# Moving small DMAs between queues and slots: where the B/C matrix is stored, and when its rows and the convolution strips are fetched

## The chip, the cores and the metric

The kernel runs on one core of a Trainium2 chip. A core has five engines, each with its own instruction stream: TensorE (PE in the profile; PEld is its weight load), VectorE (DVE), ScalarE (ACT), GpSimd (POOL) and SyncE (SP), which here only issues DMAs. Every stream runs in order and waits on semaphores that other streams or landed DMAs raise. The metric is the device time of one execution in microseconds; the kernel before takes 27,648.13 us (median of three runs, 27,644.12 to 27,659.78).

## The reference

The input is 8 images of 64 channels and 128x128 pixels, float32. Layer 0 runs a bidirectional selective scan (Mamba) over every row and over every column, averages the four results, normalises by groups of channels and adds the input. Layer 1 is a residual block of two 3x3 convolutions with batch normalisation. The scan of one sequence, cut to what matters:

```
x, z  = split(in_w @ seq);  x = silu(causal_conv(x))
dt, B, C = split(xp_w @ x)            # B and C: 16 states each
delta = softplus(dt_w @ dt + dt_b)
for t:                                # per channel d (128) and state n (16)
    h[d,n] = exp(delta[t,d] * A[d,n]) * h[d,n] + delta[t,d] * x[t,d] * B[t,n]
    y[t,d] = sum_n h[d,n] * C[t,n]
y = (y + x * D) * silu(z);  out = out_w @ y
```

Forward and reversed sequences give `f` and `r`, and the layer takes 0.5 * (f + r).

## The kernel before, in words

**Units and slots.** The work of layer 0 is cut into 512 units: 8 images, for each 32 units of four rows (`o == 0`, units 0 to 31 of an image) and 32 units of four columns (`o == 1`, units 32 to 63). A unit has 512 time steps times 128 channels times 16 states times 2 directions. It is cut into 16 slots `r`; a slot treats 64 channels (`half`), 4 states (`ng`) and one direction (`d`), so that 128 partitions hold 32 channels times 4 states and two channel quarters lie side by side: tiles of 128x1024. `where(r)` gives half, state group and direction.

**What a slot does.** `decay` (ScalarE, L350): a copy of zeros at the sequence edges and two Exp of 128x508 give `dA` in PSUM; there are two such tiles, so a slot's decay waits for the scan two slots back. `drive` (L362): `s = du * B`, on VectorE with B in PSUM (`pb`, made by TensorE in `b_rows`), or, in slots 2, 5, 9, 12 and 15 (`GPS`), on GpSimd with B in an SBUF tile `bt` that a DMA fetched (`b_tile`). `scan` (VectorE, L370): the recurrence as one instruction. `weigh` (GpSimd, L379): `s = s * C`, with C in an SBUF tile `c`. `add_up` (TensorE) folds the states, four slots later.

**What feeds a unit.** `prepare(g, before)` is a generator that makes the next unit's inputs in pieces, one piece in each of slots 0 to 6 and 8 to 13 of the current unit. Piece 9 (slot 9) makes `du = delta * x` on VectorE (L287) and `dl = delta` on ScalarE and stores both to DRAM with eight DMAs of 128 KB (`keep`, L282). Pieces 10 to 13 read them back, replicated over the four states: `replicate(g, half, d)` (L314) issues two loads of 512 KB, one `dl` and one `du`, into a pool of five tiles each. The order is (0,0), (1,0), (0,1), (1,1), in slots 10 to 13. In slot 11 ScalarE copies B and C out of PSUM (`bc`, L299) and SyncE stores that tile of 128 KB to DRAM (`bd`, L301), ahead of the second pair. From `bd` come the `bt` tiles (256 KB, a row broadcast to 32 partitions) and the `c` tiles. `c_rows` (L329) loads both directions of a state group at once: four loads of 512 KB per unit into two tiles.

**Order.** The main loop (L538 on) is written out by hand; nothing reorders it. A wait that heads SyncE's queue holds everything behind it. In the kernel before, `fetch(s + 7)` issues a `bt` load seven slots ahead and `fetch_c(s + 3)` a `c` load three slots ahead of its first use. In slot order SyncE's queue is thus: slot 9, the eight stores and a `c`; 10, first pair; 11, `bd`, second pair, `bt` of slot 2; 12, third pair; 13, fourth pair and a `c`; 14, `bt` of slot 5; then 1, `c`; 2, `bt`; 5, `bt` and `c`; 8, `bt`. The `bt` of slot 2 is the first load that reads the new `bd`.

**Normalisation and first convolution.** They run inside the row units of the next image. `normalize` (units 1 to 16) takes 512 columns per unit: slot 5 loads `xr`, slot 7 adds on GpSimd (L443) and SyncE stores `x1_d` (L444). `conv1` makes one output tile per unit from unit 5 on, in slots 14, 15, 0, 1 and 2: three groups of matmuls, the copy and store of the result (`cs`, L488 and L489), statistics. Its input strips (two SBUF tiles, two or more loads of x1_d rows each, `strip_of`) are loaded one tile ahead, at the start of the tile before, in slot 14. After the last image both run outside the loop (L590 to L597), then come the second convolution and the output.

Of the kernel before, what the change touches and what calls it, by code (L numbers as in the profile page):

```python
# [9 lines left out]
F32 = mybir.dt.float32  # L10
# [5 lines left out]
P = 128  # L16
# [3 lines left out]
N = 512  # L20
# [12 lines left out]
def tile_mamba2d_then_resblock(ctx: ExitStack, tc: tile.TileContext, x, par, gn, p_w, o_w, new_p, bn, cst, out):  # L33
# [169 lines left out]
    with ExitStack() as st:  # L203
# [42 lines left out]
        def prepare(g, before):  # L246


            w = wt[g["o"]]
            if g["o"] == 1:  # L250
                g["xc"] = work.tile([P, SEQ, HH], F32, name="xc", bufs=1)
                i = SEQ * g["i"]
                nc.scalar.copy(g["xc"], xt.rearrange("p h w -> p w h")[:, i : i + SEQ, :])
            yield
            cp = psm.tile([P, 2, N], F32, name="cp", tag="pt")
            for d in range(2):
                for s in range(NTAP):
                    j = NTAP - 1 - s
                    project(
                        cp[:, d, :], [w["wc"][:, 0, j, :], w["wc"][:, 1, j, :]], g,  # L260
                        s if d == 0 else -s, s == 0, s == NTAP - 1,
                    )
                    if s % 2:
                        yield
            u = work.tile([P, 2, N], F32, name="u")
            nc.scalar.activation(u, cp, AF.Silu, bias=w["conv_b"])  # L266
            if before is not None:
                nc.scalar.activation(before["sz"], before["sz"], AF.Silu)
            g["u"] = u
            yield  # L270
            dp = psm.tile([P, 2, N], F32, name="dp", tag="pt")
            for d in range(2):
                nc.tensor.matmul(dp[:, d, :], w["wd"], u[:, d, :], start=True, stop=True)  # L273
            yield
            nc.scalar.activation(dp, dp, AF.Softplus, bias=w["dt_b"])
            yield
            dd = g["dd"] = scratch.tile([2, 2, 32, NQ, N], F32, name="dd")

            def keep(k, v):

                for q in range(NQ):
                    nc.sync.dma_start(  # L282
                        out=dd[k, :, :, q, :].rearrange("d c t -> c d t"), in_=v[32 * q : 32 * (q + 1)]
                    )

            du = work.tile([P, 2, N], F32, name="du", tag="nat")
            nc.vector.tensor_mul(du, dp, u)  # L287
            dl = work.tile([P, 2, N], F32, name="dl", tag="nat")
            nc.scalar.copy(dl, dp)  # L289
            keep(1, du)  # L290
            keep(0, dl)
            yield
            bp = psm.tile([P, 2, N], F32, name="bp", tag="pt")
            for d in range(2):
                nc.tensor.matmul(bp[0 : 2 * NS, d, :], w["wbc"], u[:, d, :], start=True, stop=True)  # L295
            replicate(g, 0, 0)
            yield
            bc = work.tile([2 * NS, 2, N], F32, name="bc", tag="nat")
            nc.scalar.copy(bc, bp[0 : 2 * NS])  # L299
            bd = scratch.tile([2 * NS, 2, N], F32, name="bd")  # L300
            nc.sync.dma_start(out=bd, in_=bc)  # L301
            g["bd"] = bd
            replicate(g, 1, 0)
            yield
            replicate(g, 0, 1)
            yield
            zp = psa.tile([P, N], F32, name="zp", tag="b")
            project(zp, [w["wz"][:, 0, :], w["wz"][:, 1, :]], g, 0, True, True)
            g["sz"] = work.tile([P, N], F32, name="sz")
            nc.scalar.copy(g["sz"], zp)  # L310
            replicate(g, 1, 1)
            yield
# [13 lines left out]
            ng, k = divmod(r, 4)  # L326
            return k % 2, ng, k // 2

        def c_rows(g, ng):  # L329

            t = rep.tile([P, 2, N], F32, name="c", bufs=2)
            src = g["bd"][NS + 4 * ng : NS + 4 * ng + 4].rearrange("n d t -> n (d t)")
            nc.sync.dma_start(out=t.rearrange("p d t -> p (d t)"), in_=src.partition_broadcast(32))
            g["c", ng] = t

        def b_tile(g, r):

            half, ng, d = where(r)
            t = rep.tile([P, N], F32, name="bt", bufs=3)
            nc.sync.dma_start(out=t, in_=g["bd"][4 * ng : 4 * ng + 4, d, :].partition_broadcast(32))  # L340
            g["bt", r] = t
# [36 lines left out]

        def weigh(g, r):  # L379
            half, ng, d = where(r)  # L380
            s, c = g["s", r], g["c", ng][:, d, :]
            nc.gpsimd.tensor_mul(s, s, c.unsqueeze(1).to_broadcast([P, 2, N]))  # L382

        def skip(g):
# [62 lines left out]
        def strip_of(b, t, k):  # L447

            x1 = x1_d[b].rearrange("p (h w) -> p h w", w=W)
            strip = strips[k % 2]  # L450
            for e in range(2):
                es = slice(e * C, (e + 1) * C)
                rows = [2 * SEQ * t + 2 * j - e for j in range(SEQ + 1)]
                for hf in range(2):
                    js = [j for j, r in enumerate(rows) if hf * HH <= r < (hf + 1) * HH]
                    if js:
                        r = rows[js[0]] - hf * HH
                        nc.sync.dma_start(
                            out=strip[es, js[0] : js[-1] + 1, 1 : W + 1],
                            in_=x1[hf * C : (hf + 1) * C, r : r + 2 * len(js) - 1 : 2, :],  # L460
                        )

                if rows[0] < 0:
                    nc.vector.memset(strip[es, 0, :], 0.0)
                if rows[-1] >= W:
                    nc.vector.memset(strip[es, SEQ, :], 0.0)

        def conv1(b):


            order = [0, 1, 9, 2, 10, 3, 11, 4, 12, 5, 13, 6, 14, 7, 15, 8]
            strip_of(b, order[0], 0)
            st1 = small.tile([P, NT, 6], F32, name="st1", bufs=1)
            yield
            for k, t in enumerate(order):
                if k + 1 < NT:
                    strip_of(b, order[k + 1], k + 1)
                ps = psm.tile([P, 2, N], F32, name="cps", tag="pt")[:, 0, :]
                for kw in range(3):
                    for blk in range(2):  # L480
                        nc.tensor.matmul(  # L481
                            ps.rearrange("p (r w) -> p r w", w=W), w1[:, blk, kw, :],
                            strips[k % 2][:, blk : blk + SEQ, kw : kw + W],
                            start=(kw == 0 and blk == 0), stop=(kw == 2 and blk == 1),
                        )
                    yield
                cs = work.tile([P, N], F32, name="cs", tag="tok", bufs=3)
                nc.scalar.copy(cs, ps)  # L488
                nc.sync.dma_start(out=c1_d[b][:, t * N : (t + 1) * N], in_=cs)  # L489
                yield  # L490
                nc.vector.bn_stats(st1[:, t, :], cs)
                if k == NT - 1:
                    nc.sync.dma_start(out=st1_d[:, b], in_=st1)
                yield
# [16 lines left out]
        def at(s):  # L511
            return gs[s // UN], s % UN

        def fetch(s):
            if s < total and s % UN in GPS:
                b_tile(*at(s))

        def fetch_c(s):
            if s < total and s % 4 == 0:
                g, r = at(s)  # L520
                c_rows(g, where(r)[1])

        def ahead(r):

# [2 lines left out]
        with tc.manual_schedule():  # L527
            load_image(0)
            for _ in prepare(gs[0], None):
                pass  # L530
            fetch_c(0)
            fetch_c(4)
            for s in range(7):
                fetch(s)
            decay(*at(0))
            b_rows(*at(0))
# [1 line left out]
            for s in range(total + UN):  # L538
# [20 lines left out]
                    nc.scalar.activation(gs[n]["sz"], gs[n]["sz"], AF.Silu)  # L559
                if s % 2 == 0 and s + 2 < total:  # L560
                    b_rows(*at(s + 2))
                if r in CONV and n % PER > 5 or r >= CONV[0] and n % PER == 5:
                    next(conv3, None)
                if r in PREP:
                    next(pieces, None)
# [3 lines left out]
                    add_up(*at(s - LAG))  # L569
                if r in NORM and n % PER:  # L570
                    next(norm, None)
                fetch(s + 7)
                fetch_c(s + 3)
                if r == OUT and prev:
                    if n % PER == 5:
                        next(conv3, None)
                    output = emit(prev)
                    next(output)
                elif r == OUT + 1:
                    next(output, None)  # L580
                    if n % PER == 0 and prev:
                        for _ in conv3:
                            pass
                        norm = normalize(prev["b"], stats.pop(prev["b"]))
                        next(norm)
                        conv3 = conv1(prev["b"])
                elif r == 8 and live and n % PER == PER - 2 and gs[n]["b"] + 1 < B:
                    load_image(gs[n]["b"] + 1)
# [152 lines left out]
```

## Time and profile before

One profiled execution took 27,638.15 us, of which the span from the first to the last instruction is 27,636.0 us.

| what | value |
|---|---|
| median of three runs | 27,648.13 us |
| profiled execution, its span | 27,638.15 us, 27,636.0 us |
| VectorE busy | 26,018.6 us (94%) |
| GpSimd busy | 25,128.0 us (91%) |
| PE matmul busy | 19,347.3 us (70%) |
| ScalarE busy | 18,349.8 us (66%) |
| DMA | 4871.45 MB, mean 176 GB/s; SyncE's queue 52.8% of the 16 DMA engines' time |
| scan, each (L375, L377) | 2278 and 2280 ns, 8192 in all |
| drive on VectorE (L367) | 1200 ns, 5632 in all |
| drive on GpSimd (L367) | 2365 ns, 2560 in all |
| weigh on GpSimd (L382) | 2364 ns, 8192 in all |

Busy time is a union, so overlapping ends of neighbours count once. The idle time in a group's row is what its engine waited just before those instructions, with what ended most of it. A row "X <- DMA a<-b" means that the last thing to arrive was that load. SyncE (SPq) has no busy time; its waits are told by a view of their own.

### The profile page before, as it was taken

What the parts mean: (1) busy time and instruction counts of PE and PEld (TensorE: products, weight loads), DVE (VectorE), ACT (ScalarE), POOL (GpSimd) and SP (SyncE); (2) the same over time, 40 slices, a digit from 0 to 9 for tenths busy, and PEclk for the clock granted to TensorE, in tenths of its full rate; (3) what the DMA queues carried; (4) which work ended last, traced back from release to release, by engine and by line L of the source; (5) the groups of instructions that cost most, each with busy time, mean ns of one, the idle gap of its engine ahead of it and who ended that gap; (6) DMA issues with size and microseconds to landing.
All of it is one profiled execution on the core that took longest, in us unless ns stands there. A gap on an engine that the chain in (4) does not pass through costs nothing.

```text
span 27636.0 us, 232983 instructions
## 1 busy us (share of the span) xinstructions
PE 19347.3 (70%) x65068; PEld 6675.0 (24%) x65068; DVE 26018.6 (94%) x16145; ACT 18349.8 (66%) x30638; POOL 25128.0 (91%) x10916
## 2 busy tenths in 40 slices
PE   6766677666776667766676667766677666776676
PEld 1222222222222222222222222222222222222222
DVE  8999999999999999999999999999999999999942
ACT  5766666666676666766667666666667666666632
POOL 7999999999999999999999999999999999999930
PEclk8888888888888888888888888888888888888888
DMA  5555555555555555555555555555555555555545
GB/s 177 173 173 173 177 183 180 173 174 178 185 175 173 172 182 185 175 173 170 183 185 173 174 176 178 184 171 176 175 185 182 170 176 176 186 176 171 172 141 188
DMA packets 1861563, 4871.45 MB, mean 176 GB/s; under 512 B 240272, under 2 KB 387872, under 8 KB 1844384
## 3 DMA queue, kind: packets, MB, share of 16 engines
q1 hardware_dynamic: 1839664, 4754.93, 52.8%
q10 hardware_dynamic: 15984, 68.06, 0.9%
q0 software_dynamic: 4608, 33.56, 0.3%
q8 instruction: 513, 8.40, 0.1%
q14 instruction: 794, 6.50, 0.1%
HBM read 4116.04 MB, written 738.98 MB: 176 GB/s over the span
## 4 chain that ended last, share of the span: by engine, by line
DVE 40%; issue 21%; PE 17%; DMA 10%; ACT 8%; POOL 2%; SPq 1%; DVEq 0%; POOLq 0%; ACTq 0%
DVE s L367 14%; DVE s L375 12%; DVE s L377 10%; DMA du<-dd 7%; PE pb L347 6%; ACT dA L358 4%; PE yp L398 3%; PE cps L650 2%; PE dp L273 2%; PE bp L295 2%; DVE du L287 2%; POOL s L382 1%; DVE y L405 1%; DMA bt<-bd 1%; PE cp L241 1%
## 5 line engine op out<-in xcount | busy, mean ns | idle before, releaser
L382 POOL TENSOR_TENSOR s<-s,c 128x1024 f32<-128x1024 f32 x8192 | 19121.0, 2364 | 1104.3 <-DMA c<-bd 440.6
L358 ACT ACTIVATE dA<-dl,A 128x508 f32<-128x508 f32 x16384 | 11274.9, 688 | 616.4 <-DMA dl<-dd 101.1
L347 PE MATMUL pb<-u,wb 128*128 128x512 f32 x8192 | 5419.6, 748 | 7657.6 <-DVE s L367 7313.1
L377 DVE TENSOR_TENSOR_SCAN s<-dA,s 128x1024 f32<-128x1024 f32 x4096 | 9296.2, 2280 | 52.3 <-ACT dA L358 40.5
L375 DVE TENSOR_TENSOR_SCAN s<-dA,s 128x1024 f32<-128x1024 f32 x4096 | 9287.2, 2278 | 0.0
L367 DVE TENSOR_TENSOR s<-du,pb 128x1024 f32<-128x1024 f32 x5632 | 6757.8, 1200 | 559.0 <-DMA du<-dd 452.1
L367 POOL TENSOR_TENSOR s<-du,bt 128x1024 f32<-128x1024 f32 x2560 | 6055.3, 2365 | 317.3 <-DMA bt<-bd 140.6
L355 ACT COPY dA<-zeros 128x8 f32<-128x8 f32 x8192 | 1349.0, 165 | 6360.6 <-DVE s L377 4676.1
L398 PE MATMUL yp<-s,fold 128*32 128x512 f32 x32768 | 5386.2, 671 | 5.3 <-POOL s L382 5.3
L347 PEld LDWEIGHTS pb<-u,wb 128*128 128x128 f32 x8192 | 1468.9, 216 | 10579.4 <-DVE s L367 5372.1
L235 PE MATMUL cp<-xt,wc 128*128 128x512 f32 (+3 forms) x4096 | 2063.2, 628 | 132.7 <-DMA xt<-x_h 76.0
L241 PE MATMUL cp<-xc,wc 128*128 128x256 f32 (+3 forms) x8192 | 2095.3, 401 | 0.0
L241 PEld LDWEIGHTS cp<-xc,wc 128*128 128x128 f32 x8192 | 1607.4, 202 | 1038.2 <-issue 459.6
L398 PEld LDWEIGHTS yp<-s,fold 128*32 128x32 f32 x32768 | 821.7, 115 | 3451.8 <-issue 2080.6
L295 PE MATMUL bp<-u,xpT 128*32 128x512 f32 x2048 | 1636.7, 948 | 4.8 <-ACT dl L289 4.8
L358 ACT ACT_TABLE_LOAD x1030 | 1321.5, 1283 | 20.3 <-DMA dl<-dd 2.3
L235 PEld LDWEIGHTS cp<-xt,wc 128*128 128x128 f32 x4096 | 782.2, 202 | 1469.4 <-issue 1116.2
L273 PE MATMUL dp<-u,wd 128*128 128x512 f32 x2048 | 1017.3, 621 | 1.2 <-ACT u L266 1.2
L299 ACT COPY bc<-bp 32x1024 f32<-32x1024 f32 x512 | 513.1, 1002 | 744.4 <-PE yp L398 677.0
L388 PE MATMUL yp<-u,dg 128*128 128x512 f32 x2048 | 961.9, 592 | 1.2 <-DVE y L405 1.2
L679 POOL DMA_DIRECT2D out<-cc x32 | 17.2, 537 | 975.6 <-ACT cc L678 975.6
L481 PE MATMUL cps<-strip,w 128*128 128x512 f32 x1536 | 754.4, 618 | 134.3 <-DMA strip<-x_d 128.0
(107 smaller groups left out, 10117.9 us busy)
## 6 DMA issues: line engine op xcount, KB each, us to landing
c<-bd SPq DMA_DIRECT2D x2049, 512.0 KB, 4.8
dl<-dd SPq DMA_DIRECT2D x2048, 512.0 KB, 6.5
du<-dd SPq DMA_DIRECT2D x2048, 512.0 KB, 7.4
bt<-bd SPq DMA_DIRECT2D x2560, 256.0 KB, 4.7
dd<-du SPq DMA_DIRECT2D x2048, 128.0 KB, 2.3
dd<-dl SPq DMA_DIRECT2D x2048, 128.0 KB, 2.4
bd<-bc SPq DMA_DIRECT2D x512, 128.0 KB, 5.4
c_d<-cs SPq DMA_DIRECT2D x256, 256.0 KB, 5.2
```

The lines of the kernel that those rows point to most:

```text
L235: nc.tensor.matmul(ps[:, :, lo:hi], lhsT[hf], xt[:, r : r + SEQ, lo - s : hi - s], start=start, stop=stop)
L241: nc.tensor.matmul(ps[:, :, lo:hi], lhsT[hf], g["xc"][:, :, lo - s - hf * HH : hi - s - hf * HH], start=start and hf == 0, stop=stop and h ...
L273: nc.tensor.matmul(dp[:, d, :], w["wd"], u[:, d, :], start=True, stop=True)
L295: nc.tensor.matmul(bp[0 : 2 * NS, d, :], w["wbc"], u[:, d, :], start=True, stop=True)
L347: nc.tensor.matmul(pb, wt[g["o"]]["wb"][:, P * ng : P * (ng + 1)], g["u"][:, d, :], start=True, stop=True)
L355: nc.scalar.copy(dA[:, :, :, edge], zeros)
L358: nc.scalar.activation(dA[:, j, :, t], dl[:, j, :, t], AF.Exp, scale=wt[g["o"]]["A"][:, 2 * half + j, ng : ng + 1])
L367: engine.tensor_mul(s, g["du", half, d], b.unsqueeze(1).to_broadcast([P, 2, N]))
L375: nc.vector.tensor_tensor_scan(s, a, s, 0.0, ALU.mult, ALU.add)
L377: nc.vector.tensor_tensor_scan(s[:, ::-1], a[:, ::-1], s[:, ::-1], 0.0, ALU.mult, ALU.add)
L382: nc.gpsimd.tensor_mul(s, s, c.unsqueeze(1).to_broadcast([P, 2, N]))
L398: nc.tensor.matmul(g["yp"][32 * q : 32 * (q + 1), :], fold, s[:, j, :], start=False, stop=r == UN - 2, skip_group_check=True,)
```

## The change

Four edits:

- B and C are stored to DRAM by ScalarE's DMA queue, behind the copy that makes them, and no longer by SyncE.
- `c` comes in eight loads of 256 KB per unit, one per state group and direction, into five tiles of half the size (before: four of 512 KB into two).
- `fetch` places all `bt` and `c` loads: `bt` of slot 2 six slots ahead (slot 12, behind the third replica pair; before: slot 11), `bt` of slot 5 four slots ahead (slot 1; before: slot 14), the other three as before. `c` of slots 0 and 2 four slots ahead (slots 12 and 14), the other six five slots ahead (slots 15, 1, 3, 5, 7 and 9).
- The convolution starts one unit later (unit 6, slot 12, where two strips are loaded); from then on a strip is loaded two tiles ahead, with the statistics in slot 2.

The order of instructions on GpSimd is unchanged; on TensorE and VectorE only the convolution moves, by one unit; ScalarE gets 512 DMA issues.

```diff
             bd = scratch.tile([2 * NS, 2, N], F32, name="bd")
-            nc.sync.dma_start(out=bd, in_=bc)
+            nc.scalar.dma_start(out=bd, in_=bc)
...
-        def c_rows(g, ng):
-
-            t = rep.tile([P, 2, N], F32, name="c", bufs=2)
-            src = g["bd"][NS + 4 * ng : NS + 4 * ng + 4].rearrange("n d t -> n (d t)")
-            nc.sync.dma_start(out=t.rearrange("p d t -> p (d t)"), in_=src.partition_broadcast(32))
-            g["c", ng] = t
+        def c_rows(g, r):
+
+            half, ng, d = where(r)
+            t = rep.tile([P, N], F32, name="c", bufs=5)
+            src = g["bd"][NS + 4 * ng : NS + 4 * ng + 4, d, :]
+            nc.sync.dma_start(out=t, in_=src.partition_broadcast(32))
+            g["c", ng, d] = t
...
             strip_of(b, order[0], 0)
+            strip_of(b, order[1], 1)
...
-                if k + 1 < NT:
-                    strip_of(b, order[k + 1], k + 1)
...
                 nc.vector.bn_stats(st1[:, t, :], cs)
+                if k + 2 < NT:
+                    strip_of(b, order[k + 2], k + 2)
...
         def fetch(s):
-            if s < total and s % UN in GPS:
-                b_tile(*at(s))
-
-        def fetch_c(s):
-            if s < total and s % 4 == 0:
-                g, r = at(s)
-                c_rows(g, where(r)[1])
+
+
+            for k in range(8):
+                r = (s + k) % UN
+                if s + k < total and r in GPS and k == (6 if r == GPS[0] else 4 if r == GPS[1] else 7):
+                    b_tile(*at(s + k))
+                if s + k < total and r % 2 == 0 and k == (4 if r < 4 else 5):
+                    c_rows(*at(s + k))
...
-                if r in CONV and n % PER > 5 or r >= CONV[0] and n % PER == 5:
+                if r in CONV and n % PER > 6 or r >= CONV[0] and n % PER == 6:
                     next(conv3, None)
...
-                fetch(s + 7)
-                fetch_c(s + 3)
+                fetch(s)
                 if r == OUT and prev:
-                    if n % PER == 5:
+                    if n % PER == 6:
                         next(conv3, None)
```

## The prediction

> **What bounds the kernel now.** I read the page first, then the waits by engine, the busy time by stretch, SyncE's own waits, and last the timeline of single units.
>
> ```profile
> PE 19347.3 (70%) x65068; PEld 6675.0 (24%) x65068; DVE 26018.6 (94%) x16145; ACT 18349.8 (66%) x30638; POOL 25128.0 (91%) x10916
> ...
> L367 DVE TENSOR_TENSOR s<-du,pb 128x1024 f32<-128x1024 f32 x5632 | 6757.8, 1200 | 559.0 <-DMA du<-dd 452.1 <-PE pb L347 83.9 <-PE cp L235 6.5
> ```
>
> VectorE is the bound. In the unit loop its idle time is almost all in one group, the drive, and most of that waits for a `du` load. The waits give the count, and GpSimd's largest:
>
> ```profile
> DVE s L367 <- DMA du<-dd: 452.1, 253, 11.2
> POOL s L382 <- DMA c<-bd: 440.6, 264, 4.3
> ```
>
> Cut to the third image, busy time per stretch (us, PE, PEld, DVE, ACT, POOL, clock, DMA share, GB/s): units 7 to 16, which carry normalisation and convolution, and column units 32 to 62.
>
> ```profile
> 7052.80:7584.10 531.30, 397.15 (x1240) 122.40 (x1240) 499.09 (x301) 362.03 (x611) 497.37 (x220) 0.90 0.59 186
> ...
> 8346.10:9933.80 1587.70, 1083.24 (x4030) 415.72 (x4030) 1580.63 (x990) 1087.97 (x1831) 1513.35 (x653) 0.84 0.53 175
> ```
>
> The column half is full (1580.63 of 1587.70): nothing can be won there. All gain must come from row units. The same cut of the waits puts VectorE's wait for `du` at 3.2 us in units 1 to 4, 2.3 in 5 and 6 (plus 11.1 for TensorE, which stands behind the first strip), 28.7 in 7 to 16, 9.8 in 17 to 21, 10.8 in 22 to 31 and 2.5 in 32 to 62. The first image, without normalisation or convolution, has 36.1.
>
> Why is `du` late? SyncE's own waits:
>
> ```profile
> SPq L333 <- POOL s L382: 7367.1, 967, 12.0
> ...
> SPq L340 <- DMA bd<-bc: 1918.8, 511, 5.7
> ```
>
> The first is harmless: SyncE runs ahead and waits for a free `c` tile. The second is in every unit: `bt` of slot 2 stands at the queue's head until `bd` has landed. SyncE in unit 12 of the third image:
>
> ```profile
> 7351.66 1.99 SPq L282 DMA_DIRECT2D dd<-du  x4
> ...
> 7358.64 0.53 SPq L301 DMA_DIRECT2D bd<-bc  x1
> 7359.27 0.51 SPq L319 DMA_DIRECT2D dl<-dd  x1
> 7359.83 2.33 SPq L319 DMA_DIRECT2D du<-dd  x1
> 7366.56 0.51 SPq L340 DMA_DIRECT2D bt<-bd  x1
> ...
> 7369.11 0.55 SPq L319 DMA_DIRECT2D du<-dd  x1
> ```
>
> `bd` takes 7.9 us, SyncE stands still, and the fourth pair's `du` goes out at 7369.11. VectorE meets it in the drive of slot 3 of the next unit:
>
> ```profile
> 7377.88 1.22 DVE L367 TENSOR_TENSOR s<-du,pb 128x1024 f32<-128x1024 f32 x1 [2.69 <-DMA du<-dd]
> ```
>
> It landed 8.7 us after its issue and 26.2 us after the first store.
>
> **What the Trainium skill says.** "DMA: Bandwidth & Descriptors", section "Issuing engines are not separate DMA queues": DMAs of all engines share the same 16 DMA engines; another issuer saves issue time only. Its section "Queues, rings and completion order" adds that SP and ACT each own a row of rings, between which a DMA engine goes round at packet granularity. So a `bd` on ScalarE's row need not stand behind SyncE's backlog. The trace before has no such case; it shows 5.4 us (median) for `bd` behind the backlog and 2.4 for the `dd` stores of the same size ahead of it. "Perfetto Trace Analysis", section "DMA Instruction — HWDGE (DVE, Sync)": descriptor generation is locked for exclusive use, and the sequencer is free only after its own. The trace agrees in its first 14 us: SyncE's one-column loads of the row biases take 0.61 and 0.65 us while ScalarE issues in step with them, those of the column biases, later and alone, 0.35 and 0.43.
>
> **The change, part by part.**
>
> *`bd` on ScalarE.* SyncE loses an issue of 0.32 us and its wait for `bc`. ScalarE gains 512 issues between `bc` and the decay of slot 13, whose scan waits for it (unit 42 of the second image; ScalarE, then VectorE):
>
> ```profile
> 5588.96 1.00 ACT L299 COPY bc<-bp 32x1024 f32<-32x1024 f32 x1 [1.55 <-PE yp L398]
> 5589.87 0.15 ACT L355 COPY dA<-zeros 128x8 f32<-128x8 f32 x1
> 5590.06 1.41 ACT L358 ACTIVATE dA<-dl,A 128x508 f32<-128x508 f32 x2
> ```
> ```profile
> 5592.29 2.28 DVE L375 TENSOR_TENSOR_SCAN s<-dA,s 128x1024 f32<-128x1024 f32 x1
> ```
>
> The decay ends at 5591.47 and the scan starts at 5592.29: a margin of 0.82. ScalarE's store must wait for `bc` to end (5589.96); today the next copy starts 0.09 earlier. With 0.03 to start, 0.33 for the issue (median of ScalarE's loads at L676) and 0.10 to go on, the decay slips 0.55: hidden. Next to an issue of SyncE's it is 0.63 for the issue, so 0.85: 0.03 lost. Behind a held issue like the 2.33 above some 1 us is lost; I book that for one unit in ten: +50 us. Behind ScalarE's store stand that decay and the next, nothing else that is near its time.
>
> *The order of the loads.* `bt` of slot 2 moves behind the third pair, with the new `c` of slot 0 between. In the built program the eight DMA semaphores go round so that the third `dl` reuses that of `bd`, so it too waits for its landing; the block is not gone but depends on how fast ScalarE's row delivers. Bounds: 2.4 us (nothing in the way) to 5.4 (as now). I take 3.5. In the unit of the second image `bd` then lands at 5593.5, not 5595.3, and the third `dl` follows at once, not behind `bt`; then `du`, `c`, `bt`, `dl`, `du`, five issues of about 0.57: 5596.4 against 5597.85 before, 1.5 us earlier; 0.4 to 2.6 over the bounds. Bytes ahead of the last `du` stay equal where nothing else intrudes: the `c` at slot 9 is half as large, the other half is the new `c`. The pipe is at times empty while SyncE blocks, so most of the 1.5 us should reach the landing. Row units without normalisation wait about 1 us each. So (a): 7 x (9.8 + 10.8) + 36.1 = 180, seven eighths gone: -158.
>
> *Units 7 to 16.* SyncE waits in slot 7 for GpSimd's addition before it stores x1. Behind it stood one `bt`; now also a `c` (slot 7). The eight stores start 0.53 us later and 0.26 MB more goes ahead, 0.8 us at 333 GB/s (176 / 0.528). Of 2.9 us per unit I let half go: (b) 7 x 14.3 = -100. Both ends: nothing, or all 200. GpSimd's wait for `c`, 27.8 us in this stretch, goes too, since `c` of slot 0 is issued before the fourth pair; GpSimd is not the bound, its 2.36 us x 21 + 1.27 overlap to just under 50 us per unit against 53, so it only stops being a second brake.
>
> *`bt` of slot 5 at slot 1.* In convolution units it now stands behind the `cs` store, which waits for ScalarE, and is issued about 5 us into the unit; with 4.7 to land (page) it comes at 9.7, when GpSimd, behind two weighs, wants it at 9 to 10. Cost nil to 0.7 us on GpSimd, covered by its slack in the unit; without that cover 112 x 0.7 = 80 us. Other `c` and `bt` loads run far ahead: five tiles free up four slots before the issue. The eight `c` issues cost SyncE 4 x 0.52 more per unit, in idle time.
>
> *Strips.* The wait for the first strip stays: both first strips now go out ahead of the fourth pair in unit 6. (c) of 16.6 us per image in units 1 to 6 I take off 4: -28. (d) column half: 7 x 2.5, -15. (e) After the last image tiles with normalisation between them take 8.4 us each (matmuls start at 26617.75 and two tiles later at 26634.53), those without 6.1; prefetch two tiles ahead brings eleven near 6.5: -20.
>
> Sum: -158 - 100 - 28 - 15 - 20 + 50 = -271 on 27,638: 27,367. The median of the runs is 10 above the profiled execution: **27,380 us**.
>
> **Rivals.** *The DMA engines are the limit* (16%): the share is near full from the first store to the last `du`, and the bytes stay; earlier issue only queues longer. Left are (d), (e) and little else: 27,610. For it: 8.7 us from issue to landing, which is backlog. Against: SyncE's 4 us of silence in the middle. *Everything hidden* (10%): all 452 go, half the strip waits (42), the tail 25: -519, 27,130. *ScalarE is held* (10%, slower): place, the store before the decay of slot 13; price, 512 units times what exceeds 0.82. At 1.57 us per issue (longest at L676) the decay slips 1.79, 0.97 lost each: 497 - 321 = +176, 27,820. It decides from an issue of 1.23 us on (0.63 x 512 = 321). For it: SyncE's own issues are held up to 2.5 us behind its earlier ones; against: ScalarE has one small store per unit.
>
> **How the numbers follow.** Forecast 60%, own range 27,290 to 27,500 (the bounds of (a) and (b)); the rivals as given; 4% for what I do not see. Low end 27,200, high 27,640. Within 0.2% (55 us) is about what a measurement of this kernel can tell from no change. Faster: forecast, everything hidden, and two thirds of the DMA case, 0.80. Same 0.09, slower 0.11.
>
> **What would show it.** Right: the SyncE wait for `bd` falls from 1918.8 us to under 700; VectorE's wait for `du` to 150 to 250; GpSimd's for `c` under 150; `bd` lands in under 4 us; the scan of slot 13 hardly waits for ScalarE. Wrong: a new VectorE wait for `dA` (ScalarE held), `du` as late as before (DMA limit), or GpSimd waiting for `bt`.

## The result and the profile after

The change made the kernel slower: 27,824.14 us against 27,651.19 (medians of six runs each), a ratio of 1.0061 with a 95% interval of 1.0048 to 1.0074. The forecast was 27,380 with a range of 27,200 to 27,640. One execution below, the first of e2, ran in a slow state (36,615 us at a granted clock of 0.599) and is left out of every ratio.

The profiled execution took 27,831.14 us, its span is 193.4 us longer than before. The scans end at 26,714.6 us (26,509.8 before) and start at the same time, so the unit loop lost 205 us; the part behind it takes 1,114.7 us instead of 1,126.2.

The page of the kernel after, its first part and the two drive groups:

```profile
PE 19338.4 (69%) x65068; PEld 6652.0 (24%) x65068; DVE 26015.8 (93%) x16145; ACT 18400.1 (66%) x30638; POOL 25145.8 (90%) x10916
...
L368 DVE TENSOR_TENSOR s<-du,pb 128x1024 f32<-128x1024 f32 x5632 | 6752.6, 1199 | 761.0 <-DMA du<-dd 634.0
L368 POOL TENSOR_TENSOR s<-du,bt 128x1024 f32<-128x1024 f32 x2560 | 6070.5, 2371 | 918.3 <-DMA bt<-bd 754.9
```

VectorE does the same work in the same time. Its wait for `du` has grown from 452.1 to 634.0 us, which is nearly all of the loss. GpSimd has a wait for `bt` that it hardly had (140.6 before, 131.4 of it once, at the start). That was one of the prediction's signs of being wrong, but it does not reach VectorE, which waits for GpSimd's drive for 2.5 us in all (3.9 before). GpSimd's wait for `c` went from 440.6 to 18.5 us, worth nothing while `du` is late.

Busy time per stretch of the third image, as in the prediction (us, PE, PEld, DVE, ACT, POOL, clock, DMA share, GB/s): units 7 to 16, then units 32 to 62.

```profile
7121.20:7655.50 534.30, 403.59 (x1256) 124.07 (x1256) 499.62 (x301) 362.71 (x611) 500.03 (x221) 0.89 0.59 186
...
8431.40:10024.80 1593.40, 1081.22 (x4030) 420.33 (x4030) 1579.33 (x990) 1092.66 (x1831) 1512.32 (x652) 0.86 0.53 174
```

Even the column half, where "nothing can be won", lost 5.7 us. VectorE's wait for `du` by place, over all images, added up from the trace (us):

| units | before | after |
|---|---|---|
| first image, rows | 45.3 | 84.3 |
| 1 to 6 | 52.1 | 74.1 |
| 7 to 16 | 207.9 | 133.6 |
| 17 to 21 | 59.4 | 60.4 |
| 22 to 31 | 62.4 | 155.8 |
| 32 to 62 | 25.0 | 123.4 |

SyncE's own wait, which should have fallen from 1918.8 us to under 700:

```profile
SPq L319 <- DMA bd<-bc: 3424.4, 512, 9.0
```

It is no longer the `bt` load that waits for the stored B and C but the third pair's `dl`, and 6.7 us per unit instead of 3.8. That `dl` reads nothing of the store. But the DMAs of SyncE and ScalarE carry eight semaphore numbers in the trace, and the store and this `dl` have the same one in all 511 units that are prepared in the loop. The reason for the longer wait is in the timeline of unit 26 of the third image, a plain row unit; first SyncE, then ScalarE, then the drive of slot 3 in the next unit on VectorE (start, duration, engine, line, operation, output and input):

```profile
8162.43 0.52 SPq L319 DMA_DIRECT2D dl<-dd  x1
8163.01 0.59 SPq L319 DMA_DIRECT2D du<-dd  x1
8163.70 0.54 SPq L319 DMA_DIRECT2D dl<-dd  x1
8164.30 0.59 SPq L319 DMA_DIRECT2D du<-dd  x1
8171.57 0.51 SPq L319 DMA_DIRECT2D dl<-dd  x1
```
```profile
8163.53 1.00 ACT L299 COPY bc<-bp 32x1024 f32<-32x1024 f32 x1 [0.98 <-DMA dd<-dl]
8164.56 0.31 ACTq L301 DMA_DIRECT2D bd<-bc  x1
8164.91 0.17 ACT L356 COPY dA<-zeros 128x8 f32<-128x8 f32 x1 [0.39 <-ACT bc L299]
```
```profile
8182.43 1.22 DVE L368 TENSOR_TENSOR s<-du,pb 128x1024 f32<-128x1024 f32 x1 [1.73 <-DMA du<-dd]
```

Before, SyncE stood at `bd` until the copy was done, and the second pair came behind it in every unit. Now nothing holds SyncE there: the second pair goes out at 8163.70 and 8164.30, both ahead of the store at 8164.56. Its `dl` is ahead in 489 of the 511 units, its `du` in 419. The store lands later, and the third pair stands still until 8171.57, 7.0 us after the store was issued. The store's time from issue to landing, before and after (KB each, median us):

```profile
bd<-bc SPq DMA_DIRECT2D x512, 128.0 KB, 5.4
bd<-bc ACTq DMA_DIRECT2D x512, 128.0 KB, 6.8
```

What this costs can be read from the DMA packets. In units 22 to 31 of images 2 to 8, counted from the unit's first `dd` store, the 16 DMA engines of the kernel before are never busy for less than 76% of a microsecond, on average, between 1 and 24 us: while SyncE stands still, they work through the second pair. In the kernel after, the second pair has nearly landed when the third is released, and the share falls to 23% from 14 to 15 us and to 38% from 15 to 16 us. From 1 us to the landing of the last `du` the engines are idle for 3.53 us instead of 1.87, and that `du` lands 1.44 us later.

### The profile page after: what moved, and what is told of

The parts are those of the page before. It is cut to its first block, busy times and chain, and to the rows that moved or that the text cites. A ratio compares the mean times of both kernels' runs of the same rounds, so it can differ in the third digit from the quotient of the medians.

```text
span 27829.4 us, 235862 instructions
## 1 busy us (share of the span) xinstructions
PE 19338.4 (69%) x65068; PEld 6652.0 (24%) x65068; DVE 26015.8 (93%) x16145; ACT 18400.1 (66%) x30638; POOL 25145.8 (90%) x10916
## 4 chain that ended last, share of the span: by engine, by line
DVE 39%; issue 21%; PE 14%; DMA 14%; ACT 8%; SPq 2%; POOL 1%; DVEq 0%; ACTq 0%; POOLq 0%
DVE s L368 14%; DMA du<-dd 11%; DVE s L376 11%; DVE s L378 11%; PE pb L348 4%; ACT dA L359 4%; PE cps L650 2%; PE yp L399 2%; PE dp L273 2%; DVE du L287 2%; PE bp L295 2%; POOL s L383 1%; DVE y L406 1%; ACT L359 1%; SPq L319 1%
## 5 line engine op out<-in xcount | busy, mean ns | idle before, releaser
L378 DVE TENSOR_TENSOR_SCAN s<-dA,s 128x1024 f32<-128x1024 f32 x4096 | 9293.8, 2279 | 50.8 <-ACT dA L359 40.5
L368 DVE TENSOR_TENSOR s<-du,pb 128x1024 f32<-128x1024 f32 x5632 | 6752.6, 1199 | 761.0 <-DMA du<-dd 634.0
L295 PE MATMUL bp<-u,xpT 128*32 128x512 f32 x2048 | 1567.4, 911 | 4.8 <-ACT dl L289 4.8
```

The lines of the kernel that those rows point to most:

```text
L368: engine.tensor_mul(s, g["du", half, d], b.unsqueeze(1).to_broadcast([P, 2, N]))
L378: nc.vector.tensor_tensor_scan(s[:, ::-1], a[:, ::-1], s[:, ::-1], 0.0, ALU.mult, ALU.add)
```

## The experiments

In this table all times are us after the first `dd` store, means over units 22 to 31 of images 2 to 8, worked out from the issues and landings in each trace (landings: from the 40 to 48 of these 70 units for which the trace has them). "Second dl" and so on are the loads of the replica pairs. The ratio is to the kernel before, measured on the same chip. A "point" below is one hundredth of the kernel before's time. The letters A to F are the theories that the expectations name.

| kernel | second dl issued | B/C store issued, landed | third dl issued | bt of slot 2 issued | fourth dl issued | last du landed | ratio |
|---|---|---|---|---|---|---|---|
| before | 7.85 | 7.42, 12.60 | 13.26 | 12.70 | 14.63 | 23.91 | 1 |
| after | 6.16 | 7.34, 14.21 | 14.30 | 16.17 | 16.88 | 25.35 | 1.0061 |
| e1 store only | 6.16 | 7.41, 14.89 | 15.44 | 14.88 | 16.79 | 26.20 | 1.0196 |
| e8 all but store | 7.72 | 7.29, 11.95 | 8.97 | 12.55 | 13.41 | 22.26 | 0.9808 |
| e3 store behind pair | 6.23 | 7.63, 15.56 | 8.96 | 16.12 | 16.83 | 24.99 | 1.0023 |
| e4 store early | 6.19 | -8.84, -6.71 | 7.43 | 10.35 | 11.15 | 21.59 | 0.9945 |
| e5 bt only | 7.72 | 7.28, 12.96 | 9.06 | 12.93 | 13.54 | 21.68 | 0.9829 |
| e6 c only | 7.78 | 7.36, 11.99 | 12.54 | 11.98 | 14.57 | 23.94 | 0.9953 |
| e7 strips only | 7.77 | 7.35, 12.70 | 13.33 | 12.77 | 14.69 | 24.00 | 0.9953 |
| e9 pair held back | 7.88 | 7.31, 11.80 | 11.92 | 13.78 | 14.62 | 23.47 | 0.9875 |
| e10 store behind decay | 6.17 | 8.25, 15.27 | 8.96 | 16.53 | 17.23 | 24.79 | 0.9972 |

**e1: the store alone.**

```diff
 # the kernel before
-            nc.sync.dma_start(out=bd, in_=bc)
+            nc.scalar.dma_start(out=bd, in_=bc)
```

> Only the B/C store moves to ScalarE; all loads as in the kernel before. Theory A (overtaken): SyncE no longer waits for the B/C copy before the second replica pair, so 1 MB of that pair is queued ahead of the store, which then lands about 6.8 us after its issue (5.4 before); the bt load at the head of SyncE waits for it, the last du lands about 1 us later than before (25 against 23.9 us after the first dd store in plain row units), VectorE's wait for du rises from 452 to 600-750 us, time 27750-27850. Rival B (ScalarE's ring is slow by itself): the same here. Rival C (the eight c loads and the moved bt loads are what costs): no change, 27620-27680.

Measured: 28,222.35 us, 1.0196 (1.0182 to 1.0210). That is theory A's direction, but far beyond its size: it had 27,750 to 27,850 us and a wait for `du` of 600 to 750 us. The page's `bd` row and drive group:

```profile
bd<-bc ACTq DMA_DIRECT2D x512, 128.0 KB, 7.4
```
```profile
L367 DVE TENSOR_TENSOR s<-du,pb 128x1024 f32<-128x1024 f32 x5632 | 6761.5, 1201 | 1097.7 <-DMA du<-dd 972.5
```

The wait for `du` has more than doubled. Moving the store is harmful by itself. Rival C, which expected no change, falls; A and B are not told apart.

**e2 and e8: everything but the store.**

```diff
 # the kernel after
-            nc.scalar.dma_start(out=bd, in_=bc)
+            nc.sync.dma_start(out=bd, in_=bc)
```

> The change with the B/C store back on SyncE, between first and second pair; everything else as in the kernel after. Theory A and rival B: the store lands again about 5.3 us after its issue, the third pair does not wait for it, the last du lands near 23.2, VectorE's wait for du 250-400 us, time 27480-27600. Rival C: the cost stays, 27780 or more, GpSimd's wait for bt stays above 500 us.

> The change with the B/C store on SyncE once more, for a profile at the usual TensorE clock. Theory A: the store lands within 5.5 us of its issue, third pair issued right behind the second (dl near 10 us after the first dd store), last du landed at 22.8 or earlier, VectorE's wait for du under 60 us, 1.7 to 2.0 per cent faster than before.

Measured: 27,162.33 us, 0.9812 (0.9799 to 0.9826), and again 27,156.74, 0.9808 (0.9795 to 0.9822). The first was far faster than A and B had it (27,480 to 27,600); the expectation for the second was written with that time known, and came true in every figure. One line undone takes the kernel from 0.6% slower to 1.9% faster than before: the fastest version here. SyncE in unit 26 of the third image:

```profile
7926.51 0.59 SPq L319 DMA_DIRECT2D du<-dd  x1
7928.79 0.32 SPq L301 DMA_DIRECT2D bd<-bc  x1
7929.20 0.51 SPq L319 DMA_DIRECT2D dl<-dd  x1
7929.76 0.62 SPq L319 DMA_DIRECT2D du<-dd  x1
7930.43 0.59 SPq L319 DMA_DIRECT2D dl<-dd  x1
7931.07 0.60 SPq L319 DMA_DIRECT2D du<-dd  x1
7932.05 0.51 SPq L334 DMA_DIRECT2D c<-bd  x1
```

SyncE waits 1.7 us for the copy; then store, second pair and third pair go out in a row, and `c` of slot 0 waits 0.4 us for the landing. So the last `du` is in time nearly everywhere (11.4 of the 25.2 us are one wait at the start):

```profile
DVE s L368 <- DMA du<-dd: 25.2, 22, 11.4
```

**e3: on SyncE, but behind the second pair.**

```diff
 # the kernel after
-            nc.scalar.dma_start(out=bd, in_=bc)
             g["bd"] = bd
             replicate(g, 1, 0)
+            nc.sync.dma_start(out=bd, in_=bc)
```

> The change with the B/C store on SyncE but issued behind the second pair. Theory A: which queue issues it does not matter, only what is ahead of it: it lands no earlier than in the kernel after (14 us or later after the first dd store), c of slot 0 and everything behind it on SyncE are as late as there, time 27750-27880. Rival B: on SyncE's ring it lands 5.4 us after its issue (about 13 us), the time is that of the run with the store between the pairs, under 27620.

Measured: 27,756.28 us, 1.0023 (1.0012 to 1.0034), the low edge of A's range and far from B's. The page's row, with the store back on SyncE's queue:

```profile
bd<-bc SPq DMA_DIRECT2D x512, 128.0 KB, 7.8
```

Against e8 only the order of the store and the second pair differs; it costs 2.15 points. ScalarE's queue isn't needed for the harm.

**e4: the store before everything.**

```diff
 # the kernel after: in prepare, behind u
             g["u"] = u
+            bp = psm.tile([P, 2, N], F32, name="bp", tag="pt")      # and its two matmuls
             yield
+            bc = work.tile([2 * NS, 2, N], F32, name="bc", tag="nat")  # copy, bd, store on ScalarE
             dp = psm.tile([P, 2, N], F32, name="dp", tag="pt")
...                                    # the same lines are gone from slots 10 and 11
```

> The change, but B and C are computed and copied before delta (slots 5 and 6) and stored by ScalarE in slot 6, long before the dd stores; no load waits for the store. Theory A: SyncE's wait for bd falls from 3424 us to under 200, the last du lands at 22.5 or earlier, VectorE's wait for du under 200 us, time 27350-27520. Rival D (the DMA engines are the limit from the first store to the last du): the loads go out earlier but the last du still lands at 23.5 or later, time 27600 or more.

Measured: 27,529.32 us, 0.9945 (0.9933 to 0.9958), just above A's range. Its waits by engine:

```profile
DVE s L368 <- PE pb L348: 375.1, 619, 10.4
...
DVE s L368 <- DMA du<-dd: 16.4, 10, 11.6
```
```profile
bd<-bc ACTq DMA_DIRECT2D x512, 128.0 KB, 1.9
```

No wait for the store is left in SyncE's list. The last `du` lands 3.8 us earlier than in the kernel after, where rival D, the DMA engines as the limit, had it at 23.5 or later; D falls. On ScalarE's queue, with little ahead of it, the store lands in 1.9 us, so that queue isn't slow by itself (B falls). The gain is eaten elsewhere: the matmuls of B and C now stand ahead of those that make `pb` for slot 8, and they wait for `u` (536.1 us in TensorE's waits, where the kernel before has no such row), so that slot's drive starts 0.5 us late in 511 units: 255 of the 375.1 us for which VectorE waits for `pb`. That cost came with the place the piece was put in, not with the early store. It is most of the 368 us by which the unit loop is longer than in e8.

**e5, e6, e7: the other parts, one at a time.** Each is one edit in the kernel before: `bt` of slot 2 behind the third pair; `c` in eight loads into five tiles; the strips.

```diff
 # e5: fetch, called with s instead of s + 7
-            if s < total and s % UN in GPS:
-                b_tile(*at(s))
+            for k in range(6, 8):
+                if s + k < total and (s + k) % UN in GPS and k == (6 if (s + k) % UN == GPS[0] else 7):
+                    b_tile(*at(s + k))
 # e6: c_rows and the c lines of fetch as in the kernel after
 # e7: conv1 and the two "n % PER" conditions as in the kernel after
```

> The kernel before with one edit: the bt load of slot 2 goes out behind the third replica pair instead of the second. Theory A: this alone takes the wait for the B/C store out of the third pair's way, so the third pair leaves about 4 us earlier, the last du lands at about 23.2 or earlier after the first dd store, VectorE's wait for du falls from 452 to 100-250 us: 0.5 to 1.2 per cent faster than before. Rival E (the gain of the run without ScalarE's store comes from c in eight loads): no change or slower.

> The kernel before with one edit: c in eight loads of 256 KB into five tiles, fetched in the slots of the change; bt loads, store and strips as before. Theory A: GpSimd's wait for c falls from 441 to under 150 us, but the bt load that waits for the store still stands ahead of the third pair and c of slot 0 adds an issue ahead of the fourth: the last du is up to 0.6 us later, time 0.1 to 0.6 per cent slower than before. Rival E: 0.5 per cent faster or more.

> The kernel before with one edit: convolution from unit 6 on, strips two tiles ahead. Both theories: the wait for the first strip stays, the tail after the last scan is about 12 us shorter, time 10 to 50 us less than before (up to 0.2 per cent).

Measured: e5 27,214.54 us, 0.9829 (0.9816 to 0.9843); e6 27,558.38, 0.9953 (0.9940 to 0.9965); e7 27,560.96, 0.9953 (0.9940 to 0.9967). SyncE's wait in e5, and the drive group:

```profile
SPq L340 <- DMA bd<-bc: 1204.6, 510, 4.2
```
```profile
L367 DVE TENSOR_TENSOR s<-du,pb 128x1024 f32<-128x1024 f32 x5632 | 6726.7, 1194 | 140.0 <-PE pb L347 70.2
```

`du` is no longer what it waits for most (50.9 us are left): one `bt` load behind the third pair instead of ahead of it is nearly the whole gain. That is theory A's side, and more than it expected; rival E falls, though e6 comes close to its mark. e6 and e7 were both expected wrongly. In e6 the `c` load that stands ahead of the first pair is half as large, and the store lands in 4.4 us, not 5.4. It seems that this pays for the extra issue ahead of the fourth pair: the last `du` is as late as before in plain row units. In units 7 to 16 VectorE's wait for it falls from 207.9 to 149.0. In e7 the same wait falls to 94.5: the strip loads, before issued right behind the fourth pair, are gone from there. The fourth `du` of these units goes out 0.1 us earlier than before and takes 8.7 us to land, not 9.1 (means over the 44 of 70 units whose landing the trace has). That it is the strips' bytes which held it back fits this, but is not shown. The three gains add up to 2.65 points; together (e8) they give 1.92, since after e5 only 51 us of waiting for `du` are left. The later `bt` of slot 5 was not run alone.

**e9: the store on ScalarE, but the second pair held back.**

```diff
 # the kernel after
-            replicate(g, 1, 0)
+            replicate(g, 1, 0, bc)
...
                 t = rep.tile([P, 2, N], F32, name=what, bufs=5)
+                if touch is not None and k == 0:
+                    nc.scalar.copy(t[0:1, 0, 0:1], touch[0:1, 0, 0:1])
```

> The kernel after, but SyncE is held from the second replica pair until ScalarE has issued the store: behind the store ScalarE writes one element of the dl tile that this pair loads. The store stays on ScalarE's queue, and the third dl still waits for its landing. Theory A: without the second pair ahead of it the store lands within 5 us of its issue (about 12 us after the first dd store, 14.2 in the kernel after), third pair and all behind it about 2 us earlier, last du landed at 23.8 or earlier, 0.1 to 1.3 per cent faster than before. Rival F (what costs is ScalarE's queue: its issue ahead of a decay, or its row of rings): no change from the kernel after, 0.4 to 0.8 per cent slower than before, or worse, since ScalarE has one instruction more.

Measured: 27,334.73 us, 0.9875 (0.9862 to 0.9889), with all that A expected.

```profile
bd<-bc ACTq DMA_DIRECT2D x512, 128.0 KB, 4.3
```
```profile
DVE s L370 <- DMA du<-dd: 166.9, 171, 11.8
```

Queue, issue ahead of the decay, the semaphore shared with the third `dl` and the order of the other loads are those of the kernel after, apart from one ScalarE copy of a single element; only the second pair goes out behind the store. That gives 1.86 of the 2.53 points between the kernel after and e8. F, which expected no change, falls. The remaining 0.67 is what separates e9 from e8: the third pair still waits for the landing (11.92 against 8.97 us), with the queue as the other difference.

**e10: the store behind the decay of slot 13.**

```diff
 # the kernel after
-            nc.scalar.dma_start(out=bd, in_=bc)
             g["bd"] = bd
             replicate(g, 1, 0)
             yield
             replicate(g, 0, 1)
+            nc.scalar.dma_start(out=bd, in_=bc)
```

> The kernel after, but ScalarE issues the store behind the decay of slot 13 instead of ahead of it; in the built program the third du (not the third dl) then waits for the store. Theory A: the store is issued 1.5 us later and lands 0.5 to 1.5 us later than in the kernel after, the last du too, 0.8 to 1.4 per cent slower than before. Rival F (ScalarE's issue holds the decay): that decay is free again, at least 0.2 points better than the kernel after.

Measured: 27,606.87 us, 0.9972 (0.9962 to 0.9981). Theory A missed this clearly, and F's mark was reached. The store did land 1.06 us later, as A said. But F's mechanism is not there. VectorE's waits:

```profile
DVE s L368 <- DMA du<-dd: 430.2, 282, 11.6
...
DVE s L378 <- ACT dA L359: 42.6, 112, 0.4
```

The wait for the decay is 40.5 us in the kernel after, and as much before, so it did not fall. The 204 us come from `du`. The store now has the semaphore of the third `du` (in all 511 units), which waits until 15.33 us. The third `dl` goes out at 8.96 instead of 14.30 us, and less is queued when the stop ends. So the shared semaphore is a second cause, and a large one while the store is late; A had left it out of this run's numbers. Its exact share stays open: in e3 the third `dl` and `du` are both free and the fourth pair leaves 0.4 us earlier than in e10, yet the last `du` lands 0.2 us later and the ratio is 0.5 points worse. The DMA engines had moved 6.88 MB by that landing in e3 and 6.61 in e10; why is not shown.

## Why the prediction was wrong

**The step that failed** is in "The order of the loads": "how fast ScalarE's row delivers. Bounds: 2.4 us (nothing in the way) to 5.4 (as now). I take 3.5." Measured: 6.8. The upper bound took for granted that the same bytes would stand ahead of the store. Two paragraphs earlier the text had noted that "SyncE loses an issue of 0.32 us and its wait for `bc`" and had counted it as a saving only. That wait also kept 1 MB of the second pair behind the store. Without it the landing moves from 12.60 to 14.21 us, and the third `dl` waits for it. Instead of 1.5 us earlier, the fourth `du` goes out 2.26 us later in plain row units (17.54 against 15.28).

The same sum has a sign wrong. With the store landing after 5.4 us, at 5595.4, five issues of 0.57 bring the fourth `du` to 5598.25. That is 0.4 us later than the 5597.85 of before, and not 0.4 earlier, as "0.4 to 2.6 over the bounds" has it: the text's own upper bound was already a loss, and its range of times held none. And the ground for passing the gain on to the landing, that "The pipe is at times empty while SyncE blocks", is not in the trace before, where the DMA engines' share stays at 76% or more between 1 and 24 us; the pipe runs empty in the kernel after.

**What the cited page also says.** The Trainium skill's page "DMA: Bandwidth & Descriptors", section "Queues, rings and completion order", from which the prediction took that the two rows are served in turn, also says that a DMA's semaphore increment lands only after every earlier write of that DMA engine, across its queues. No run here shows whether this rule or the sharing of the engines sets the store's time: it lands at 14.21 us, behind the `dl` (13.94) and ahead of the `du` (15.27) of the pair issued ahead of it. The held issue, for which the prediction cited the Trainium skill's "Perfetto Trace Analysis", section "DMA Instruction — HWDGE (DVE, Sync)", does not show in the kernel after: in 316 of the 512 units the store's issue overlaps one of SyncE's, and its median is 309 ns there and 308 in the others. (The prediction's reading of the first 14 us is not exact: the loads of the column biases were not "alone", since an issue of ScalarE's at 14.76 us overlaps both.)

**Step by step.** (a) Row units without normalisation, -158: the waits for `du` in units 17 to 31 and the first image rose by 133 instead. (b) Units 7 to 16, -100: -74 of the wait for `du`, but the wait for the first strip, 74.5 us in units 5 and 6, is now in unit 7 and as large (76.2), so (c), -28, brought nothing either. (d) The column half, -15: +98; its slack of about 1.2 us (last `du` landed at 23.88, needed by the drive of slot 3 at 25.05) was smaller than the delay of 1.25 us. (e) The tail, -20: -11.5. ScalarE's holds, +50: none. The store's issue is 309 ns in the median and never over 380, and the wait for a decay stays at 40.5 us. GpSimd's `c` (under 150: 18.5) and `bt` of slot 5 (nil to 0.7 per unit: 19.1 us in all) came as told.

**The rivals.** "ScalarE is held" had the right time, 27,820, by luck, from a mechanism that did not occur. "Everything hidden", 27,130, is what the change does without its first edit (27,157). "The DMA engines are the limit" had read the share rightly as near full, but fell with e4: the last `du` could land earlier. Once no stop hurts, it does hold: in e4, e5 and e8 the engines are busy for 99% or more of every microsecond from 13 to 21 us (the units and the count of the table), and the last `du` lands just behind that. None of the rivals was the one that came: that the edit meant to take a wait away takes an order away with it.

**The sizes.** e5 shows that the moved `bt` load is worth 473 us, where (a) and (b) together had 258. The halving in (b) was too careful: in e5 the last `du` lands 2.2 us earlier in plain row units, not 1.5, and nearly every wait for it goes, those of units 1 to 6 (52.1 us before) and of the column half (25.0) with them. e7 shows 127 us for the strips, where (c) and (e) had 48, since their loads were costed only where their own tiles waited and not by what they delay.

## What to carry to other kernels

A wait at the head of a DMA queue does two things: it delays what stands behind it, and it keeps that behind something. Before a small store is moved to another engine's queue, list the loads that the old wait kept back; if they are large and others wait for the store's landing, the store loses more than the queue gains. First try to move the load that does the waiting: here that was one load, one slot later, and 1.7%. And look at the DMA engines' share during the stop: a stop with loads in flight costs less than one after they have landed.

## What the runs showed of the hardware

A store of 128 KB on ScalarE's queue landed after 1.9 us with little ahead of it (e4), after 4.3 behind the first pair (e9), and after 6.8 and 7.4 where 1 MB more from SyncE's queue was issued in the same 2 us (after, e1). The other queue let it pass some of that, not all: it landed 1.1 us ahead of the second pair's `du`, whereas on SyncE's own queue (e3) it landed 0.4 us behind it. While SyncE stood still with a pair in flight, the DMA engines were busy for 82% or more of every microsecond (before, 8 to 13 us after the first `dd` store); where the pair had nearly landed when the stop ended (after), they fell to 23% for a microsecond. And 512 more DMA issues on ScalarE, 0.31 us each, cost VectorE nothing that can be seen: its wait for a decay lies between 40.5 and 42.6 us in every run in which the order of TensorE's and ScalarE's other work is the same.
